# Sixty-one groups of edges fetched by hand instead of fifty-seven, with one semaphore a buffer: a graph network layer on one Trainium2 core

## The chip, the cores and the metric

The kernel runs on one core of one Trainium2 chip. The metric is the time of the whole program on the device, in microseconds (us). A profiled execution has a span as well: the time from its first to its last instruction.

A core has five engines with instruction queues of their own: TensorE (PE, with its weight loads shown as PEld), VectorE (DVE), ScalarE (ACT), GpSimd (POOL) and SyncE (SP). SyncE computes nothing; it issues DMAs. Engines wait for each other by semaphores.

## What is computed

A layer of a graph network over 12,500 nodes with 128 features and 400,000 edges with 32 features, the edges sorted by their target node. The reference, cut to its core:

```python
h = jnp.maximum(_layernorm(x, axis=-1), 0.0)
s, d = src, dst                                      # of 400,000 edges, sorted by d
e = jnp.concatenate([h[s], h[d], edge_attr], axis=-1)
m = jax.nn.relu(e @ w1 + b1) @ w2 + b2
agg = jax.ops.segment_sum(m, d, num_segments=12500)
gi = agg @ w_ih + b_ih
gh = h @ w_hh + b_hh
r, z = sigmoid(i_r + h_r), sigmoid(i_z + h_z)
n = tanh(i_n + r * h_n)
out = x + (1.0 - z) * n + z * h
```

## The kernel before

**Stages.** First the nodes are normalised. The kernel keeps `h` transposed in SBUF (`hT_all`, one column of 128 numbers a node) and writes two products to DRAM: `A = h @ w1[0:128]`, the part of the source node, and `B = h @ w1[128:256] + b1`, the part of the target node. Then the edges pass in 391 groups (`NP`) of up to eight tiles of 128 edges (`PAIR = 8`; 1,024 edges). A group is worked in two units, and the main loop at the end of the kernel runs over the 782 units `u`; a unit of group `k` is `2k` or `2k + 1`.

**One group.** TensorE adds two parts of an edge's row in PSUM (`pre`, L663 on): the target's row of `B` (chosen by a one-hot matrix that `onehot_T` makes from the target numbers) and the edge features. The third part, the source's row of `A`, comes in one of three ways:

- *Gathered.* `gather` (L148) issues eight indirect DMAs on GpSimd, one a tile of 128 rows, into a buffer `G`. There are eleven such buffers (`GBUFS`), taken in a ring, so a gather refills the buffer of the gathered group eleven places earlier, once that one has been used. `add` (L687) adds `G` to PSUM on VectorE, with a floor at zero, and writes `RB` (L701). The first nine groups (`RAW`) are gathered from `x` itself, since `A` isn't ready then; they are normalised here, by VectorE and ScalarE (`raw_stats`, `raw_fin`, `raw_h`, `raw_turn`).
- *As columns.* `one_by_one` copies the columns of the 1,024 source nodes out of `hT_all`, one by one, on ScalarE (`"act"`, L960) or, two at a time with a byte copy behind each 128, on VectorE (`"dve"`, L967 and L972). Each column's place is a register, loaded in lots of 16 or 32 (L945). TensorE then multiplies these columns by `w1[0:128]` (L684), and ScalarE's `relu` writes `RB` (L710).
- *As rows.* SyncE issues one small DMA a row (`"sp"`, L952) from `A` into a buffer `G_sp`, of which there is one. `add` then treats it as a gathered group.

`RB` is summed into target nodes by TensorE (`seg`, L724), with a one-hot of each edge's place in a window of 32 nodes as the weights. `onehot` (L606 on) makes this for one group with one comparison on VectorE (L623), into one of six buffers.

**Who fetches which group.** `SPREAD` says how many groups go to the three engines by hand and `START` the unit in which each engine's first job begins. The list of places runs from `START // 2 + 2` to `NP` less a number for each engine, evenly spaced. Before, VectorE has 27 groups (22, 36, ... 370, 384), ScalarE 28 (17, 31, ... 372, 386) and SyncE 2 (196 and 379); the other 334 are gathered. A job's columns or rows are spread evenly over the units from the job before it to its own group, less four units (eight for SyncE): `run_jobs` issues a part of them in each of four phases of a unit.

**Order.** The order on each engine is written out by hand in the main loop. A unit issues gathers (`gathers`), window rows and loads on SyncE, a part of the jobs, `stages(u)` (which works ahead: the one-hots for three groups later, `pre` for unit `u + 3`, `add` and `relu` for unit `u + 2`), and `seg(u)`. Every engine works through its queue in order.

**Semaphores.** The library gives each DMA a semaphore out of eight lanes for GpSimd's DMAs and eight for SyncE's, in turn. A DMA waits until the DMA before it in its lane has landed. VectorE's add waits for the eight lanes of its group's eight gathers, and for TensorE.

Of the kernel before, what the change touches and what calls it, by code (L numbers as in the profile page):

```python
# [55 lines left out]
SPREAD = {"dve": 27, "act": 28, "sp": 2}  # L56
START = {"dve": 14, "act": 4, "sp": 24}
# [6 lines left out]
def tile_gnn(ctx: ExitStack, tc: tile.TileContext, x, src, srcT, dstT, dstP, eaT, eaP, w1, b1, w2T, b2,  # L64
# [27 lines left out]
    for m, n in SPREAD.items():  # L92
        lo, hi = START[m] // 2 + 2, NP - {"dve": 7, "act": 5, "sp": 12}[m]
        for i in range(n):
            k = lo + int((i + 1) * (hi - lo) / n)
            while k in mode:
                k += 1
            mode[k] = m
            order[m].append(k)
# [47 lines left out]

    def gather(k):  # L148
        if k >= NP or k in mode:
            return  # L150
        G[k] = gp.tile([128, GRP, 2, D], F32, name="G")
        table = x if k < RAW else A
        for u in (2 * k, 2 * k + 1):
            for t, j, a in unit_tiles(u):
                c, i = divmod(t, CH)
                nc.gpsimd.indirect_dma_start(  # L156
                    out=G[k][:, j, a, :], out_offset=None, in_=table,
                    in_offset=bass.IndirectOffsetOnAxis(ap=src_i[c][:, i:i + 1], axis=0))

# [7 lines left out]
    OHB = [const.tile([128, GRP, 2, V], F32, name=f"OH{i}") for i in range(6)]  # L167
# [438 lines left out]
    def onehot(k):  # L606
        if k >= NP:
            return
        t0, t1 = tiles(k)
        OH[k] = OHB[k % len(OHB)]  # L610
        row = SEGB[((k - 3) // 2 + 1) % 2][:, 256:256 + V]
        for a in range(2) if k == 0 else (None,):
            if a is None:
                o, s = OH[k].rearrange("p j a v -> p a j v"), slice(t0, t1)
                d = dloc[:, s].rearrange("p (a j) -> p a j", a=2)[:, :, :, None]
                shape = [128, 2, GRP, V]
                i = row[:, None, None, :]
            else:
                e = min(t1, (a + 1) * GRP)
                o, d = OH[k][:, :e - a * GRP, a, :], dloc[:, a * GRP:e, None]  # L620
                shape = [128, e - a * GRP, V]
                i = row[:, None, :]
            nc.vector.tensor_tensor(o, d.to_broadcast(shape), i.to_broadcast(shape),  # L623
                                    op=ALU.is_equal)
# [62 lines left out]
    def add(u):  # L687
        if u >= NU or u < 0:
            return
        k, h = divmod(u, 2)  # L690
        if h == 0 and k < NP - 1:
            return
        c = slice(0, PAIR) if k < NP - 1 else slice(GRP * h, GRP * h + GRP)
        o, p = RB[k % 2][:, c, :D], PP[k][:, c, :]
        if u in HE or k in hand:
            RT[u] = o, p
            HE.pop(u, None)
            HE.pop(u - 1, None)
            hand.pop(k, None)
        else:  # L700
            nc.vector._custom_dve(TENSOR_ADD_SAT, out=o, in0=p,  # L701
                                  in1=G[k].rearrange("p j a f -> p (j a) f")[:, c, :], s0=float("inf"), s1=0.0)
        if h == 1:
            PP.pop(k)
            G.pop(k, None)
# [9 lines left out]
    def seg(u):  # L715
# [218 lines left out]
    def one_by_one(m, k):  # L934
        et = {"act": ET.Activation, "dve": ET.DVE, "sp": ET.SP}[m]
        r = by_hand.index(k)
        if m == "sp":
            G[k] = pj.tile([128, GRP, 2, D], F32, name="G_sp", bufs=1)
# [4 lines left out]
        for e0 in range(0, PAIR * 128, LOAD[m]):  # L943
# [4 lines left out]
            if m == "sp":  # L948
                for i, v in enumerate(vals):
                    e = e0 + i  # L950
                    a, j = divmod(e // 128, GRP)
                    nc.sync.dma_start(rows[e % 128:e % 128 + 1, j, a, :],  # L952
                                      A_bytes[bass.ds(v, ROW)].rearrange("(o f) -> o f", o=1))
# [316 lines left out]
```

## Time and profile before

| | |
|---|---|
| time, median of 3 runs | 3408.0 us (3399.38 to 3409.23) |
| time of the profiled execution | 3403.76 us |
| span of the profiled execution | 3401.8 us |
| TensorE busy, its granted clock | 2417.4 us, 71%; 0.796 |
| VectorE busy | 2225.1 us, 65% |
| ScalarE busy | 3079.4 us, 91% |
| GpSimd busy | 2566.1 us, 75% |
| DMA, mean | 99 GB/s |

How to read the rows of such a page: a row has the line of the kernel, the engine, the operation, what it writes and reads, the shape, and how often it ran; behind the first bar stand the busy time in us and the mean duration of one in ns; behind the second the idle time of the engine just before these instructions, and what ended most of it. "issue" means that the profile shows nothing that the engine waited for. Register loads, semaphore waits and the issue of DMAs don't count as busy; in a timeline they stand with a q behind the engine's name. In a view of windows a row has the start and end of a stretch and its length, then for each engine the busy time and, in brackets, how many instructions. In a view of waits a row has who waited for whom, the total in us, how often, and the longest.

### The profile page before, as it was taken

Reading aid. Unit: us, or ns where it says so; the run is one execution under the profiler, and the core shown is the slowest. Engines: PE = TensorE matmul, PEld = TensorE weight load, DVE = VectorE, ACT = ScalarE, POOL = GpSimd, SP = SyncE. Lnnn points to the kernel's source line nnn. Section 1 sums busy time; section 2 is a strip of 40 time slices with the busy share of each in tenths; the row PEclk is TensorE's granted clock in tenths of the full one; section 3 lists DMA queues with packets and bytes.
Section 4 is the critical chain, followed back from the end, with each engine's and each line's share of the span. In section 5 each row is a group of like instructions: output and inputs, shape, how many; then the busy total and the mean of one; then the engine's idle time right before and its main releaser. Section 6 shows DMA issues by size and latency. Waiting matters only on the chain. (4 is left out here: it accounts for less than half of the span.)

```text
span 3401.8 us, 88642 instructions
## 1 busy us (share of the span) xinstructions
PE 2417.4 (71%) x13113; PEld 1563.7 (46%) x13113; DVE 2225.1 (65%) x16468; ACT 3079.4 (91%) x29057; POOL 2566.1 (75%) x2678
## 2 busy tenths in 40 slices
PE   7567777777677767776777667676677767766767
PEld 7444444444445444544444444444444434444445
DVE  8556666666676666666666666666666666666665
ACT  7699999999999998999899988988988898898984
POOL 7777777777777777777777777777777777777776
PEclk9777887887887778777877877788777778777878
DMA  6434444434443333343434433443433334343332
GB/s 213 106 88 93 97 100 99 101 94 100 102 98 94 98 99 95 95 101 97 98 93 99 98 94 93 96 96 93 98 93 92 95 94 99 92 97 96 92 92 73
DMA packets 191316, 335.44 MB, mean 99 GB/s; under 512 B 66753, under 2 KB 112384, under 8 KB 190729
## 3 DMA queue, kind: packets, MB, share of 16 engines
q0 software_dynamic: 85408, 175.09, 23.0%
q1 hardware_dynamic: 105177, 154.58, 16.4%
q14 instruction: 478, 3.92, 0.4%
q8 instruction: 109, 1.79, 0.2%
q10 hardware_dynamic: 144, 0.07, 0.0%
HBM read 309.24 MB, written 20.24 MB: 97 GB/s over the span
## 5 line engine op out<-in xcount | busy, mean ns | idle before, releaser
L156 POOL DMA_INDIRECT G<-A,src_i x2600 | 2498.9, 961 | 796.2 <-issue 753.7
L960 ACT COPY HE_act<-hT_all 128x4 uint8 x28672 | 2886.8, 189 | 51.4 <-issue 27.0
L967 DVE SCALAR_TENSOR_TENSOR both<-hT_all 128x4 uint16 x13824 | 1173.4, 153 | 988.5 <-issue 980.7
L673 PE MATMUL pre<-RW,L 128*128 128x256 f32 x3128 | 1132.4, 488 | 229.8 <-DVE RB L701 220.6
L673 PEld LDWEIGHTS pre<-RW,L 128*128 128x128 f32 x3128 | 660.6, 236 | 506.1 <-DVE RB L701 234.0
L724 PE MATMUL seg<-RB,OH 128*32 128x129 f32 x6250 | 603.9, 324 | 380.0 <-DVE RB L701 349.7
L724 PEld LDWEIGHTS seg<-RB,OH 128*32 128x32 f32 x6250 | 333.1, 125 | 820.4 <-DVE RB L701 532.7
L701 DVE CUSTOM_DVE_ANT_0 RB<-pre,G 128x1024 f32<-128x1024 f32 (+1 forms) x326 | 394.5, 1210 | 62.7 <-DMA G<-A,src_i 49.2
L575 DVE TENSOR_SCALAR L<-L,node_of 64x512 f32<-64x512 int32 x382 | 186.7, 489 | 9.7 <-DMA L<-in_dstP 9.4
L719 PE MATMUL seg<-zrow 1*128 1x129 bf16 x196 | 45.3, 231 | 164.4 <-DVE OH L623 164.2
L623 DVE TENSOR_TENSOR OH<-dloc,seg 128x256 f32<-128x256 f16 (+1 forms) x392 | 159.5, 407 | 0.5 <-issue 0.5
L750 PE MATMUL nd<-spot,sums 128*128 128x40 f32 x782 | 116.6, 321 | 1.2 <-DVE sums L733 1.2
L750 PEld LDWEIGHTS nd<-spot,sums 128*128 128x128 f32 x782 | 112.4, 231 | 10.5 <-issue 9.0
L710 ACT ACTIVATE RB<-pre 128x1024 f32<-128x1024 f32 x64 | 65.0, 1015 | 52.4 <-PE pre L684 52.4
L809 ACT ACTIVATE gt<-nd 128x512 f32<-128x512 f32 (+2 forms) x28 | 16.4, 585 | 96.5 <-PE nd L803 96.5
L972 DVE COPY HE_dve<-both 128x512 uint8<-128x512 uint8 x216 | 96.6, 447 | 7.4
L684 PEld LDWEIGHTS pre<-w1a,HE_act 128*128 128x128 f32 x448 | 88.4, 245 | 11.6
L684 PEld LDWEIGHTS pre<-w1a,HE_dve 128*128 128x128 f32 x432 | 87.9, 252 | 12.1
L684 PE MATMUL pre<-w1a,HE_act 128*128 128x128 f32 x448 | 86.4, 327 | 0.0
L684 PE MATMUL pre<-w1a,HE_dve 128*128 128x128 f32 x432 | 85.1, 333 | 0.0
L156 POOL DMA_INDIRECT G<-in_x,src_i x69 | 65.9, 954 | 21.8 <-issue 20.7
L233 PE MATMUL nd<-w1b,hT_all 128*128 128x128 f32 x224 | 45.5, 346 | 43.3 <-DVE xb L835 43.3
(177 smaller groups left out, 1383.9 us busy)
## 6 DMA issues: line engine op xcount, KB each, us to landing
L<-in_dstP SPq DMA_DIRECT2D x195, 256.0 KB
L<-in_eaP SPq DMA_DIRECT2D x195, 256.0 KB
G<-A,src_i POOLq DMA_INDIRECT x2600
G_sp<-A SPq DMA_DIRECT2D x2048, 0.5 KB
RW<-B SPq DMA_DIRECT2D x782, 16.0 KB
xb<-in_x SPq DMA_DIRECT2D x26, 256.0 KB
out<-xb SPq DMA_DIRECT2D x26, 256.0 KB
xs<-in_x SPq DMA_DIRECT2D x11, 512.0 KB
```

Of the source, the lines that this page charges most:

```text
L156: nc.gpsimd.indirect_dma_start(out=G[k][:, j, a, :], out_offset=None, in_=table, in_offset=bass.IndirectOffsetOnAxis(ap=src_i[c][:, i:i + ...
L575: nc.vector.tensor_scalar(o, i, node_of[:, k:k + 1], None, op0=ALU.is_equal)
L623: nc.vector.tensor_tensor(o, d.to_broadcast(shape), i.to_broadcast(shape), op=ALU.is_equal)
L673: nc.tensor.matmul(p[:, 2 * i:2 * i + 2, :], Ls[k // QP][:, c0:c0 + 128], RW[k % 4], start=True, stop=not raw)
L684: nc.tensor.matmul(p[:, 2 * i + a, :], cols, w1a, start=False, stop=n + 1 == len(l) or l[n + 1][1] != j)
L701: nc.vector._custom_dve(TENSOR_ADD_SAT, out=o, in0=p, in1=G[k].rearrange("p j a f -> p (j a) f")[:, c, :], s0=float("inf"), s1=0.0)
L710: nc.scalar.activation(o, p, AF.Relu)
L724: nc.tensor.matmul(p[r0:r0 + V, :D + 1], OH[k][:, j, a, :], RB[k % 2][:, 2 * j + a, :D + 1], start=False, stop=all(b != a for _, _, b in r ...
L750: nc.tensor.matmul(p[:, bass.ds(offs[i], V + SHIFT)], sums[:, slot(b, i), :D], spot[:, i % 2, :], start=False, stop=i == len(offs) - 1)
L960: nc.scalar.copy(he[:, e * 4:e * 4 + 4], column(v))
L967: nc.vector.scalar_tensor_tensor(both[:, (e0 % PIECE + i) // 2, :], column(vals[i + 1]), 256.0, column(vals[i]), op0=ALU.mult, op1=ALU.add)
L972: nc.vector.tensor_copy(he[:, p0 * 4:(p0 + PIECE) * 4].rearrange("p (n c b) -> p n c b", c=2, b=4), both.bitcast(U8).rearrange("p n (b c) ...
```

## The change

- *Fewer gathers.* VectorE takes 28 groups as columns instead of 27 and SyncE 5 groups as rows instead of 2 (87, 160, 233, 306, 379); ScalarE's number stays 28. 330 groups are gathered instead of 334.
- *Columns begin sooner and end later.* The first job of ScalarE begins in unit 2 instead of 4, that of VectorE in unit 10 instead of 14. The last groups with columns are 386 (VectorE) and 388 (ScalarE) instead of 384 and 386.
- *Semaphores of the buffers.* A gather of a group from `RAW` up to the last but one counts up a semaphore of its ring buffer (`filled`), and a row of SyncE one of its group (`brought`). These DMAs leave the lanes: they no longer wait for a lane, and the add waits for one value of one semaphore. In the order of the built program the add had waits for eight lanes and TensorE, and has one for `filled` and one for TensorE; each of SyncE's row copies had a wait for a lane, and has none.
- *One-hots of two groups at once.* One comparison writes the one-hots of groups `2i` and `2i + 1`, 512 elements a partition instead of 256, into one of three buffers of twice the size. The tiles stand in another order in it. The first group and the last have comparisons of their own.

The diff, cut to its core:

```diff
-SPREAD = {"dve": 27, "act": 28, "sp": 2}
-START = {"dve": 14, "act": 4, "sp": 24}
+SPREAD = {"dve": 28, "act": 28, "sp": 5}
+START = {"dve": 10, "act": 2, "sp": 24}
...
-        lo, hi = START[m] // 2 + 2, NP - {"dve": 7, "act": 5, "sp": 12}[m]
+        lo, hi = START[m] // 2 + 2, NP - {"dve": 5, "act": 3, "sp": 12}[m]
...
+    filled = [tc.alloc_semaphore(f"filled{i}") for i in range(GBUFS)]
+    uses, goal = [0] * GBUFS, {}
+
     def gather(k):
         if k >= NP or k in mode:
             return
+        i = ring.index(k) % GBUFS
+        if RAW <= k < NP - 1:
+            uses[i] += 1
+            goal[k] = filled[i], 16 * PAIR * uses[i]
...
-                nc.gpsimd.indirect_dma_start(
+                fetched = nc.gpsimd.indirect_dma_start(
                     out=G[k][:, j, a, :], out_offset=None, in_=table,
                     in_offset=bass.IndirectOffsetOnAxis(ap=src_i[c][:, i:i + 1], axis=0))
+                if k in goal:
+                    fetched.then_inc(goal[k][0], 16)
+                    tc.no_tile_sem_insts.add(fetched.ins.name)
+                    tc.add_to_no_dep_group(f"rows{k}", fetched.ins)
...
-    OHB = [const.tile([128, GRP, 2, V], F32, name=f"OH{i}") for i in range(6)]
+    OHB = [const.tile([128, 2 * PAIR, V], F32, name=f"OH{i}") for i in range(3)]
...
     def onehot(k):
-        if k >= NP:
+        if k >= NP or (k % 2 and k > 1):
             return
...
+        n = 2 if 1 < k < NP - 1 else 1
+        for i in range(n):
+            OH[k + i] = o[:, PAIR * ((k + i) % 2):PAIR * ((k + i) % 2) + PAIR, :]
+        t0, t1 = tiles(k)[0], tiles(k + n - 1)[1]
...
+        for p, e0, e1 in parts:
+            shape = [128, e1 - e0, V]
+            nc.vector.tensor_tensor(p, dloc[:, e0:e1, None].to_broadcast(shape),
+                                    row[:, None, :].to_broadcast(shape), op=ALU.is_equal)
...
         else:
-            nc.vector._custom_dve(TENSOR_ADD_SAT, out=o, in0=p,
+            if k in goal:
+                nc.vector.wait_ge(*goal[k])
+            made = nc.vector._custom_dve(TENSOR_ADD_SAT, out=o, in0=p,
                                   in1=G[k].rearrange("p j a f -> p (j a) f")[:, c, :], s0=float("inf"), s1=0.0)
+            if k in goal:
+                tc.declare_no_dep(made.ins, group=f"rows{k}", reason="behind the wait for the landing")
+                tc.declare_fence(made.ins, group=f"rows{k}")
...
-            nc.tensor.matmul(p[r0:r0 + V, :D + 1], OH[k][:, j, a, :],
+            nc.tensor.matmul(p[r0:r0 + V, :D + 1], OH[k][:, a * GRP + j, :],
...
         if m == "sp":
+            goal[k] = tc.alloc_semaphore(f"brought{r}"), 16 * PAIR * 128
             G[k] = pj.tile([128, GRP, 2, D], F32, name="G_sp", bufs=1)
...
-                    nc.sync.dma_start(rows[e % 128:e % 128 + 1, j, a, :],
-                                      A_bytes[bass.ds(v, ROW)].rearrange("(o f) -> o f", o=1))
+                    fetched = nc.sync.dma_start(rows[e % 128:e % 128 + 1, j, a, :],
+                                                A_bytes[bass.ds(v, ROW)].rearrange("(o f) -> o f", o=1))
+                    fetched.then_inc(goal[k][0], 16)
+                    tc.no_tile_sem_insts.add(fetched.ins.name)
+                    tc.add_to_no_dep_group(f"rows{k}", fetched.ins)
```

More of the change, by code (lines that the diff above doesn't have):

```diff
@@ L606, in onehot @@
     def onehot(k):
-        if k >= NP:
+        if k >= NP or (k % 2 and k > 1):
             return
-        t0, t1 = tiles(k)
-        OH[k] = OHB[k % len(OHB)]
+        o = OHB[(k // 2) % len(OHB)]
         row = SEGB[((k - 3) // 2 + 1) % 2][:, 256:256 + V]
[L612 to L624, printed above, removed]
+        n = 2 if 1 < k < NP - 1 else 1
+        for i in range(n):
+            OH[k + i] = o[:, PAIR * ((k + i) % 2):PAIR * ((k + i) % 2) + PAIR, :]
+        t0, t1 = tiles(k)[0], tiles(k + n - 1)[1]
+        if k:
+            parts = ((o[:, PAIR * (k % 2):PAIR * (k % 2) + t1 - t0, :], t0, t1),)
+        else:
+            parts = tuple((OH[0][:, a * GRP:min(t1, (a + 1) * GRP), :], a * GRP, min(t1, (a + 1) * GRP))
+                          for a in range(2))
+        for p, e0, e1 in parts:
+            shape = [128, e1 - e0, V]
+            nc.vector.tensor_tensor(p, dloc[:, e0:e1, None].to_broadcast(shape),
+                                    row[:, None, :].to_broadcast(shape), op=ALU.is_equal)
     def unit(u):
```

## The prediction

> **What bounds the kernel now.** I read the page first, for the engine that never rests: GpSimd (POOL), which issues the gathers.
>
> ```profile
> PE 2417.4 (71%) x13113; PEld 1563.7 (46%) x13113; DVE 2225.1 (65%) x16468; ACT 3079.4 (91%) x29057; POOL 2566.1 (75%) x2678
> L156 POOL DMA_INDIRECT G<-A,src_i x2600 | 2498.9, 961 | 796.2 <-issue 753.7
> L960 ACT COPY HE_act<-hT_all 128x4 uint8 x28672 | 2886.8, 189 | 51.4 <-issue 27.0
> ```
>
> ScalarE is the busiest by share, yet POOL is the one without slack: the pause before a gather is 796.2/2600 = 0.31 us, nearly all "issue". The view of line 156 gives the first and last start:
>
> ```profile
> L156 POOL DMA_INDIRECT G<-A,src_i x2600: 940/945/1552, 92.3 to 3383.9; - x186
> ```
>
> From 92.3 to 3383.9 + 0.95 = 3384.9 are 3292.6 us for 2600 gathers: **1.266 us each, 10.13 us for a group of eight**, with nothing between. 334 of the 391 groups are gathered.
>
> The second question is who follows whom. Two adds of VectorE (DVE) and the windows between them:
>
> ```profile
> 227.82 1.21 DVE L701 CUSTOM_DVE_ANT_0 RB<-pre,G 128x1024 f32<-128x1024 f32 x1
> 1597.41 1.22 DVE L701 CUSTOM_DVE_ANT_0 RB<-pre,G 128x1024 f32<-128x1024 f32 x1 [0.55 <-DMA G<-A,src_i]
> ...
> 228.00:1598.00 1370.00, 258.38 (x2688) 142.75 (x2688) 175.02 (x145) 24.39 (x24) 0.80 0.40 98
> ...
> 228.00:1598.00 1370.00, 1005.62 (x5429) 638.26 (x5428) 928.29 (x7054) 1310.22 (x12777) 1039.28 (x1082) 0.80 0.40 98
> ...
> DVE both L967 <- issue: 421.0, 374, 2.6
> ...
> DVE RB L701 <- DMA G<-A,src_i: 48.4, 28, 3.7
> ```
>
> The first window counts the writes of RB: 145 adds and 24 relus, so the two adds are 168 groups apart (12 and 180): 8.15 us a group. In the second, VectorE is busy 928.3 of 1370 us; it stands another 421.0 before its column work, waiting for nothing but its own register loads. That is 98.5%: **up to group 180 VectorE sets the pace**, with ScalarE at 95.6% beside it. The last row is of the time after 1598 us: now the adds wait for gathers. The consumer has caught up, and from 1597.41 to the add of group 385 at 3357.91 (below) a group takes 1760.5/205 = 8.59 us, about 10.13 x 334/391 = 8.65: **GpSimd's pace**. As GpSimd never stops in either stage, the end is its work plus a tail of 3401.8 - 3384.9 = 17 us.
>
> **The change, part by part.** *Fewer gathers.* 57 groups fetched by hand become 61 (VectorE 27 to 28, SyncE 2 to 5), so 4 groups, 32 gathers, go: 32 x 1.266 = **-40.5 us**. What was pruned from the waits gives GpSimd nothing by my reading: the earliest gathers, which have no predecessor to wait for, already run at the same 1.25 us:
>
> ```profile
> 4.67 0.94 POOL L156 DMA_INDIRECT G<-in_x,src_i  x1 [0.31 <-issue]
> 5.92 0.94 POOL L156 DMA_INDIRECT G<-in_x,src_i  x1 [0.30 <-issue]
> ```
>
> *One more column group on VectorE.* Its jobs come every 379/28 = 13.54 groups instead of 375/27 = 13.89, 2.6% denser.
>
> ```profile
> 228.00:1598.00 1370.00, 526.71 (x6204) 0.80 0.40 98
> ...
> 228.00:1598.00 1370.00, 43.57 (x97) 0.80 0.40 98
> ...
> L623 DVE TENSOR_TENSOR OH<-dloc,seg 128x256 f32<-128x256 f16 x390 | 159.1, 408 | 0.5 <-issue 0.5
> ...
> L813 DVE TENSOR_TENSOR gt<-gt,misc 128x512 f32<-128x512 f32 x26 | 17.6, 678 | 0.1
> ...
> L701 DVEq EVENT_SEMAPHORE  x1358: 21/50/2846, 201.2 to 3386.5; - x194
> ```
>
> Columns (first row), their byte copies (second) and the loads' 421.0 make 991.3/168 = 5.90 us a group; 2.6% is **+0.15**. One-hots of two groups: 2 x 0.408 becomes one of 512 elements, which no row shows; the 512-element row with an input in PSUM has 0.678, so -0.14 a pair, **-0.07** a group (bounds: nothing, if only the elements count, and -0.2, half of 0.408). The add's eight waits become one: 1358/326 = 4.2 waiting instructions of 50 ns now, one or two after, so -0.13 to 0; I take -0.06. VectorE's own pace becomes 8.15 + 0.15 - 0.07 - 0.06 = 8.17 us (8.02 to 8.30). It lies under the rest only while it stays below the gathers'.
>
> *GpSimd against VectorE.* Gathers last 961 ns in the mean, 945 in the median: 16 ns x 2600 = 42 us of lengthening.
>
> ```profile
> L575 DVE TENSOR_SCALAR L<-L,node_of 64x512 f32<-64x512 int32 x382 | 186.7, 489 | 9.7 <-DMA L<-in_dstP 9.4
> ...
> L972 DVE COPY HE_dve<-both 128x512 uint8<-128x512 uint8 x216 | 96.6, 447 | 7.4
> ```
>
> Put wholly on these 598 instructions it is 0.07 us each; the added column group brings 8 more copies: **+0.6 us**. [...]
>
> *Columns begin sooner.* ScalarE starts at unit 2 instead of 4, VectorE at 10 instead of 14 (a unit is half a group), while the first nine groups are still normalised here. ScalarE's relus mark the pace:
>
> ```profile
> 132.77 1.00 ACT L710 ACTIVATE RB<-pre 128x1024 f32<-128x1024 f32 x1
> 139.33 1.00 ACT L710 ACTIVATE RB<-pre 128x1024 f32<-128x1024 f32 x1
> 148.78 1.00 ACT L710 ACTIVATE RB<-pre 128x1024 f32<-128x1024 f32 x1
> 160.60 1.00 ACT L710 ACTIVATE RB<-pre 128x1024 f32<-128x1024 f32 x1
> ...
> 203.40 0.95 POOL L156 DMA_INDIRECT G<-A,src_i  x1 [0.72 <-DVE RB L701]
> ```
>
> Two units without columns take 6.6 us (132.77 to 139.33), with them 11.8 (148.78 to 160.60): starting two units sooner makes everything behind 5.3 us later. VectorE's four units fall where ScalarE sets the pace; I put 2 us on them (0 to 12). What is late next is GpSimd: a gather refills the buffer of eleven gathered groups ago, and at 203.40 it already waits 0.72 us for group 9's add. So there the 7 us become a stall of GpSimd in full. The first hand-fetched groups also move one or two places forward, which makes some refills depend on an add one group later (8.15 us) where a few us of margin exist: 3 more. **+10 us**, bounds 0 and 25.
>
> *Columns end later.* The last hand-fetched groups are 386 and 388 instead of 384 and 386.
>
> ```profile
> 3351.58 1.02 ACT L710 ACTIVATE RB<-pre 128x1024 f32<-128x1024 f32 x1 [2.24 <-PE pre L684]
> 3357.91 1.23 DVE L701 CUSTOM_DVE_ANT_0 RB<-pre,G 128x1024 f32<-128x1024 f32 x1
> 3366.24 1.02 ACT L710 ACTIVATE RB<-pre 128x1024 f32<-128x1024 f32 x1 [1.38 <-PE pre L684]
> 3369.43 1.22 DVE L701 CUSTOM_DVE_ANT_0 RB<-pre,G 128x1024 f32<-128x1024 f32 x1
> ...
> 3386.64 0.69 DVE L701 CUSTOM_DVE_ANT_0 RB<-pre,G 128x512 f32<-128x512 f32 x1 [3.67 <-DMA G<-A,src_i]
> ```
>
> These are groups 384 to 387 and the last add. Group 385's gathers end 32 before the last, at 3344.4, and its add comes 13.5 us behind; the groups after it have no columns, cost 3.2 us and catch up, so the last add waits for its gather. Afterwards only 24 gathers follow 385, which ends at 3384.9 - 40.5 + 10 - 30.4 = 3324.0. With a lag of 9 there (5 to 13), one group at 8.2, the stretch 386 to 388 at the 14.7 that 384 to 386 take now, and three steps of 3.2, the last add is at 3365.5, against 3386.6 - 40.5 + 10 = 3356.1 by gathers alone: **+9 us** (0 to 13).
>
> *SyncE.* Each row copy no longer waits for one of eight lanes.
>
> ```profile
> 1088.38 1.32 SPq L952 DMA_DIRECT2D G_sp<-A  x4
> 1089.87 0.81 SPq L602 DMA_DIRECT2D RW<-B  x2
> 1090.80 0.58 SPq L563 DMA_DIRECT2D L<-in_dstP  x1
> 1091.43 0.50 SPq L566 DMA_DIRECT2D L<-in_eaP  x1
> 1092.05 1.59 SPq L952 DMA_DIRECT2D G_sp<-A  x4
> ...
> L945 SPq TENSOR_LOAD <-at x64: 1876/2142/2377, 227.6 to 3229.5; - x64
> ```
>
> A job of 1024 rows now has about 68 groups: 15.1 rows x 0.33 = 5.0, their register loads 15.1/32 x 2.14 = 1.0, window rows 0.8, the half of the two L loads 0.5, some 0.3 for nodes: 7.6 of 8.5 us. It stays hidden, with 0.9 us of room a group.
>
> Sum on the profiled execution's own time (span 3401.8, time 3403.8): 3403.8 - 40.5 + 0.6 + 10 + 9 = **3383 us**. That execution lies 4 us under the median shown and inside its runs, so I leave it there.
>
> **The rivals.** *The buffers hold GpSimd throughout*: the early stall recurs at later refills and takes the upper bound, 25, with the tail's 13: 3403.8 - 40.5 + 0.6 + 38 = 3402, no change. For it: the 0.72 us wait; against: the gap between 8.17 and the new 10.13 x 330/391 = 8.55 grows margin by 0.4 us a group. *VectorE becomes the bound*: from 227.8 + 7 at group 12 to the 3324 of group 385 a pace of 8.28 suffices; above it VectorE decides. If loads find less work to hide under (421.0/387 loads = 1.09 us show now, of 2.15) and its pace is 8.45, group 385 is added at 235 + 373 x 8.45 = 3387, and with the present 44 us behind it and 2 around the span: 3433, slower.
>
> ```profile
> L945 DVEq TENSOR_LOAD <-at x864: 2095/2150/3239, 188.2 to 3336.5; - x173
> ```
>
> *SyncE becomes the bound*: from 0.385 us a row its group takes 8.5. At the other row's 1.59/4 = 0.40 it takes 8.7 over 340 groups: 235 + 340 x 8.7 + 33 x 8.15 + 46 = 3508 us. For it: 0.40 was seen; against: that row follows a large L load whose lanes it waited on. *GpSimd's 0.31 us pause is the lane wait*, and goes: then VectorE sets all, 235 + 373 x 8.17 + 46 = 3328. Against it stand the early gathers.
>
> **How the numbers follow.** Forecast 0.68, held buffers 0.10, VectorE 0.08, SyncE 0.10, pause 0.04. The forecast's own range is 3363 (no stall, no tail) to 3402. The wide one takes half of VectorE's case: 3360 to 3415; left out are 0.04, 0.04 and 0.10. Within 0.3% (10 us, about what a measurement of this kernel can tell from no change) is 3398 to 3418: half of the held buffers and a third of VectorE's case, 0.08; faster 0.77; slower 0.15.
>
> **What would show it.** Right: gathers still 1.27 us apart, 2637 of them; a new idle stretch of GpSimd of 5 to 20 us in total between 130 and 420 us; adds waiting for gathers only after group 200; the last add not waiting for its gather. Wrong: GpSimd idle beyond 420 us (buffers or VectorE), SyncE's row copies above 0.385 us with adds waiting on G_sp, or gathers closer than 1.25 us.

## The result, and the profile after

The changed kernel takes 3414.53 us (median of 15 runs, 3410.7 to 3423.64) against 3408.0 (15 runs, 3399.38 to 3409.83): a ratio of 1.0024, interval 1.0017 to 1.0031. It was forecast at 3383; it is 6.5 us slower than before. The profiled execution took 3417.5 us, its span is 3415.5.

The page of the changed kernel, first the busy times, then three groups (line 163 is the gather, 713 the add, 986 VectorE's column copies):

```profile
PE 2432.2 (71%) x13129; PEld 1567.2 (46%) x13129; DVE 2255.9 (66%) x16793; ACT 3081.9 (90%) x29058; POOL 2537.3 (74%) x2646
...
L163 POOL DMA_INDIRECT G<-A,src_i x2568 | 2470.1, 962 | 796.5 <-issue 761.1
L986 DVE SCALAR_TENSOR_TENSOR both<-hT_all 128x4 uint16 x14336 | 1213.0, 154 | 1003.3 <-issue 989.9
L713 DVE CUSTOM_DVE_ANT_0 RB<-pre,G 128x1024 f32<-128x1024 f32 x322 | 389.4, 1210 | 16.8 <-PE pre L683 16.8
```

The last row holds the answer: the adds wait 16.8 us in all, and none of it for gathered rows. Before, they waited for gathers 48.4 us after 1598 us alone. The consumer never catches up with GpSimd.

GpSimd itself did what was forecast. The view of line 163 (shortest, median and longest duration in ns, then the first and last start), and the timeline of GpSimd around the buffers' first refill:

```profile
L163 POOL DMA_INDIRECT G<-A,src_i x2568: 941/947/1812, 93.1 to 3355.5; - x198
...
196.92 1.19 POOL L163 DMA_INDIRECT G<-A,src_i  x1 [2.42 <-PE misc L666]
214.25 0.95 POOL L163 DMA_INDIRECT G<-A,src_i  x1 [7.13 <-DVE RB L713]
```

The gathers end at 3355.5 + 0.95 = 3356.4; the forecast's terms give 3384.9 - 40.5 + 10 = 3354.4. The stall is there, 7.1 us behind an add and 2.4 behind a TensorE product. (The add of group 12 comes 11.5 us later than before, at 239.27 instead of 227.82, where the forecast had 7.) But the tail behind the last gather is 3415.5 - 3356.4 = 59 us, where the forecast had 17 + 9 = 26. These 33 us are nearly the whole miss (3417.5 - 3383 = 34.5).

In the timeline of VectorE, the adds of groups 12, 176 and 378, and the last three:

```profile
239.27 1.21 DVE L713 CUSTOM_DVE_ANT_0 RB<-pre,G 128x1024 f32<-128x1024 f32 x1
1629.01 1.21 DVE L713 CUSTOM_DVE_ANT_0 RB<-pre,G 128x1024 f32<-128x1024 f32 x1
3317.20 1.22 DVE L713 CUSTOM_DVE_ANT_0 RB<-pre,G 128x1024 f32<-128x1024 f32 x1
...
3390.39 1.22 DVE L713 CUSTOM_DVE_ANT_0 RB<-pre,G 128x1024 f32<-128x1024 f32 x1 [1.51 <-PE pre L683]
3395.31 1.29 DVE L713 CUSTOM_DVE_ANT_0 RB<-pre,G 128x512 f32<-128x512 f32 x2 [3.14 <-PE pre L683]
```

The pace is (1629.01 - 239.27)/164 = **8.47 us** a group, then (3317.20 - 1629.01)/202 = 8.36. The forecast's own bound was 8.28: above it VectorE decides. The last add waits for TensorE, not for its gather.

To split the pace, I take VectorE's own work between the adds of groups 12 and 176: its busy time, and the idle time before column copies that nothing released (the loads). The window and the view of VectorE's waits, first before, with the add of group 176 ahead:

```profile
1564.69 1.21 DVE L701 CUSTOM_DVE_ANT_0 RB<-pre,G 128x1024 f32<-128x1024 f32 x1
...
227.80:1564.70 1336.90, 984.17 (x5314) 624.16 (x5314) 907.27 (x6891) 1277.94 (x12455) 1014.18 (x1056) 0.80 0.40 98
...
DVE both L967 <- issue: 409.5, 364, 2.6
```

and after, with VectorE's longest waits on other engines and TensorE's longest:

```profile
239.30:1629.00 1389.70, 1003.07 (x5314) 629.28 (x5314) 916.15 (x6974) 1269.59 (x12334) 1055.22 (x1097) 0.78 0.41 96
...
DVE both L986 <- issue: 421.2, 353, 2.6
DVE RB L713 <- PE pre L683: 14.9, 6, 3.9
DVE TOT L776 <- PE nd L765: 9.9, 2, 6.5
...
PE seg L739 <- DVE RB L713: 128.9, 72, 5.4
```

Before, (907.27 + 409.5)/164 = 8.03 us of the 8.15 are own work. After, (916.15 + 421.2)/164 = 8.16 of 8.47. So the own work grew by 0.13, and the rest, which is nearly all waiting for other engines and DMAs, from 0.12 to 0.32. For the two together the forecast had +0.02. From group 176 to 378, where before is held by the gathers, the changed kernel has 8.21 us of own work (1124.1 busy and 534.5 before columns in 202 groups) and 0.15 of waits.

### The profile page after: what moved, and what is told of

It reads as the page before. It is cut to its first block, busy times and chain, and to the rows that moved or that the text cites. A ratio compares the mean times of both kernels' runs of the same rounds, so it can differ in the third digit from the quotient of the medians.

```text
span 3415.5 us, 93943 instructions
## 1 busy us (share of the span) xinstructions
PE 2432.2 (71%) x13129; PEld 1567.2 (46%) x13129; DVE 2255.9 (66%) x16793; ACT 3081.9 (90%) x29058; POOL 2537.3 (74%) x2646
## 3 DMA queue, kind: packets, MB, share of 16 engines
q14 instruction: 518, 4.24, 0.4%
## 5 line engine op out<-in xcount | busy, mean ns | idle before, releaser
L163 POOL DMA_INDIRECT G<-A,src_i x2568 | 2470.1, 962 | 796.5 <-issue 761.1
L979 ACT COPY HE_act<-hT_all 128x4 uint8 x28672 | 2890.5, 189 | 53.9 <-issue 29.8
L986 DVE SCALAR_TENSOR_TENSOR both<-hT_all 128x4 uint16 x14336 | 1213.0, 154 | 1003.3 <-issue 989.9
L683 PEld LDWEIGHTS pre<-RW,L 128*128 128x128 f32 x3128 | 667.8, 238 | 507.4 <-issue 296.1
L739 PE MATMUL seg<-RB,OH 128*32 128x129 f32 x6250 | 616.3, 329 | 336.6 <-DVE RB L713 296.2
L713 DVE CUSTOM_DVE_ANT_0 RB<-pre,G 128x1024 f32<-128x1024 f32 x322 | 389.4, 1210 | 16.8 <-PE pre L683 16.8
L633 DVE TENSOR_TENSOR OH<-dloc,seg 128x512 f32<-128x512 f16 (+1 forms) x198 | 132.3, 668 | 0.1
L765 PE MATMUL nd<-spot,sums 128*128 128x40 f32 x782 | 125.5, 335 | 5.7 <-DVE sums L748 5.7
L765 PEld LDWEIGHTS nd<-spot,sums 128*128 128x128 f32 x782 | 121.0, 246 | 15.2 <-issue 9.0
L694 PEld LDWEIGHTS pre<-w1a,HE_dve 128*128 128x128 f32 x448 | 78.5, 219 | 8.7
L848 PE MATMUL nd<-ident,gt 128*128 128x128 f32 (+2 forms) x112 | 29.6, 412 | 71.5 <-DVE gt L844 67.1
```

The lines of the kernel that those rows point to most:

```text
L163: fetched = nc.gpsimd.indirect_dma_start(out=G[k][:, j, a, :], out_offset=None, in_=table, in_offset=bass.IndirectOffsetOnAxis(ap=src_i[c] ...
L633: nc.vector.tensor_tensor(p, dloc[:, e0:e1, None].to_broadcast(shape), row[:, None, :].to_broadcast(shape), op=ALU.is_equal)
L683: nc.tensor.matmul(p[:, 2 * i:2 * i + 2, :], Ls[k // QP][:, c0:c0 + 128], RW[k % 4], start=True, stop=not raw)
L694: nc.tensor.matmul(p[:, 2 * i + a, :], cols, w1a, start=False, stop=n + 1 == len(l) or l[n + 1][1] != j)
L713: made = nc.vector._custom_dve(TENSOR_ADD_SAT, out=o, in0=p, in1=G[k].rearrange("p j a f -> p (j a) f")[:, c, :], s0=float("inf"), s1=0.0)
L739: nc.tensor.matmul(p[r0:r0 + V, :D + 1], OH[k][:, a * GRP + j, :], RB[k % 2][:, 2 * j + a, :D + 1], start=False, stop=all(b != a for _, _, ...
```

## The experiments

Theory: VectorE's pace, raised by the 28th column group, holds the kernel. Rivals: SyncE's fuller queue (late window rows), the early beginning, or the semaphores and one-hots themselves. ScalarE, which was at 95.6% before, is busy 1269.59 of 1389.70 us in the window above, 91%, so it is not the one. The first four runs shared one chip (before: 3406.18 us there), the next four another (3399.02), so each is compared by its ratio to before. The table gives pace, own work and the rest per group from add 12 to add 176, worked out as above from unrounded figures, one profile a kernel; rows follow where a verdict rests on them.

| kernel | ratio [interval] | pace | own | waits |
|---|---|---|---|---|
| before | 1 | 8.15 | 8.03 | 0.12 |
| changed | 1.0024 [1.0017, 1.0031] | 8.47 | 8.16 | 0.32 |
| old split and places | 1.0011 [1.0002, 1.0021] | 8.14 | 7.91 | 0.22 |
| SyncE 2 groups | 1.0013 [1.0004, 1.0023] | 8.43 | 8.14 | 0.30 |
| VectorE 27 groups | 0.9940 [0.9923, 0.9956] | 8.26 | 7.89 | 0.37 |
| old beginnings and ends | 1.0020 [1.0010, 1.0029] | 8.46 | 8.25 | 0.22 |
| half the loads | 0.9915 [0.9899, 0.9932] | 8.25 | 6.35 | 1.89 |
| half of each add | 0.9915 [0.9898, 0.9931] | 8.28 | 8.01 | 0.27 |
| single one-hots | 1.0045 [1.0030, 1.0059] | 8.44 | 8.13 | 0.31 |
| gathers in lanes | 1.0184 [1.0156, 1.0211] | 8.52 | 8.27 | 0.25 |

**The semaphores and one-hots alone.** The changed kernel with

```diff
-SPREAD = {"dve": 28, "act": 28, "sp": 5}
-START = {"dve": 10, "act": 2, "sp": 24}
+SPREAD = {"dve": 27, "act": 28, "sp": 2}
+START = {"dve": 14, "act": 4, "sp": 24}
...
-        lo, hi = START[m] // 2 + 2, NP - {"dve": 5, "act": 3, "sp": 12}[m]
+        lo, hi = START[m] // 2 + 2, NP - {"dve": 7, "act": 5, "sp": 12}[m]
```

> The change's semaphores and one-hots of two groups alone; the groups by hand and their places as before (27, 28, 2). 334 groups are gathered, so GpSimd bounds the second half as before. By the prediction's own terms for these two edits (-0.07 and -0.06 us a group) the pace from group 12 to 176 falls from 8.15 to about 8.02 us, and the time stays within 6 us of before (3408). If the two edits save VectorE nothing, the pace is 8.15 again. Neither theory of the slowdown (SyncE's full queue, VectorE's further column group) expects late window rows here: TensorE's waits for RW stay under 20 us in the whole run.

Its window and waits of VectorE up to group 176, and over the whole span the wait for gathers:

```profile
228.50:1563.00 1334.50, 981.54 (x5314) 621.93 (x5314) 899.26 (x6808) 1279.10 (x12461) 1013.22 (x1052) 0.80 0.39 98
...
DVE both L986 <- issue: 398.4, 341, 2.4
DVE RB L713 <- DMA G<-A,src_i: 12.5, 5, 3.5
...
DVE RB L713 <- DMA G<-A,src_i: 107.5, 46, 6.6
```

VectorE's own work falls by 0.12, (899.26 + 398.4)/164 = 7.91, as summed, but the pace is 8.14, not the expected 8.02. This is the gathers' doing: from 1300 us on the adds wait for them (12.5 us in the window). Up to group 130 no add does, and there the pace is (1173.6 - 228.5)/118 = 8.01 against (1184.7 - 227.8)/118 = 8.11 before: 0.10 of the forecast's 0.13 arrive. ScalarE is busy 96% of the window; whether it holds the rest no run tells. In the second half the adds wait for gathers throughout, so nothing is gained. Alone these parts leave the time where it was, +0.1%.

**SyncE's queue.** The changed kernel with 2 groups on SyncE:

```diff
-SPREAD = {"dve": 28, "act": 28, "sp": 5}
+SPREAD = {"dve": 28, "act": 28, "sp": 2}
```

> The change with SyncE at 2 groups instead of 5; 333 groups are gathered. SyncE theory (rows fill its queue, window rows land late, TensorE and then VectorE wait): TensorE's waits for RW fall from 86 us to under 20, the pace from group 12 to 176 falls from 8.47 to 8.2, GpSimd becomes the bound again after some 250 groups and the time is about 3405 (gathers end near 3386, a tail of some 20). VectorE theory (its own work is too long): the pace stays at 8.4 or above and the time at 3412 to 3420.

TensorE's waits for window rows of SyncE, over the span, in this kernel:

```profile
PE pre L683 <- DMA RW<-B: 10.6, 1, 10.6
```

and in the changed kernel:

```profile
PE pre L683 <- DMA RW<-B: 85.9, 25, 10.1
```

They are gone, and the pace stays at 8.43 with the same 0.30 of waits. SyncE isn't what holds it, and three groups more to gather (30 us of GpSimd) cost no time either: GpSimd has that much room.

**VectorE's 28th group.** The changed kernel with 27 column groups:

```diff
-SPREAD = {"dve": 28, "act": 28, "sp": 5}
+SPREAD = {"dve": 27, "act": 28, "sp": 5}
```

> The change with VectorE at 27 groups instead of 28, SyncE still at 5; 331 groups are gathered. VectorE theory: the pace from group 12 to 176 falls from 8.47 to 8.25 or less, the gathers (ending near 3367) bound the end, and the time is 3385 to 3392. SyncE theory: waits for RW stay at 50 us or more, the pace stays at 8.35 or above, and the time is 3400 or more.

3385.11 us: 0.6% faster than before on the same chip, and by the ratios 0.8% faster than the changed kernel. Its window, its column copies in it (x5996; the changed kernel has 6220 in its window), the waits there and the wait for gathers over the span:

```profile
232.80:1586.90 1354.10, 978.80 (x5298) 617.75 (x5297) 893.18 (x6748) 1269.50 (x12332) 1028.13 (x1070) 0.79 0.41 97
...
232.80:1586.90 1354.10, 507.24 (x5996) 0.79 0.41 97
...
DVE both L986 <- issue: 400.2, 327, 2.6
...
DVE RB L713 <- DMA G<-A,src_i: 55.4, 27, 4.3
```

The pace drops to 8.26, under 8.28, and the adds wait for gathers again. SyncE's theory fails a second time: TensorE's waits for window rows are 172.6 us over the span, twice those of the changed kernel, and the kernel is faster. Own work falls by 8.16 - (893.18 + 400.2)/164 = 0.27 us for (6220 - 5996)/164 = 1.37 column copies a group: 0.196 us each, or 0.27/1.37 x 512 = 100 us for a job, where the forecast used the average, 5.90/36.9 x 512 = 82.

Behind this stands one profile of each kernel; with the own work of the kernel with 2 groups on SyncE, which has the same columns as the changed one, it is 0.184 us and 94.

Why the margin costs more than the average can be read from VectorE's queue. The timeline of the changed kernel, and the register loads of its column line:

```profile
1509.27 0.50 DVE L991 COPY HE_dve<-both 128x512 uint8<-128x512 uint8 x1
1511.52 1.28 DVE L986 SCALAR_TENSOR_TENSOR both<-hT_all 128x4 uint16 x16 [1.76 <-issue]
1512.72 0.47 DVE L586 TENSOR_SCALAR L<-L,node_of 64x512 f32<-64x512 int32 x1
1514.30 1.02 DVE L986 SCALAR_TENSOR_TENSOR both<-hT_all 128x4 uint16 x12 [1.10 <-issue]
...
L961 DVEq TENSOR_LOAD <-at x896: 2095/2152/3206, 176.1 to 3364.1; - x180
```

Sixteen copies take 1.28 us; then the queue loads 32 registers for 2.15. Whatever VectorE is still working on covers a part of it: here 0.47 us of line 586 stands under the second load. By this reading the cover is fixed, so a further job finds less of it; halving the adds (below) bears it out. Paid in full a job is 32 x 2.15 + 512 x 0.08 + 8 x 0.45 = 113 us. The measured 94 to 100 lie between that and 82.

**The early beginning.** The changed kernel with the beginnings and ends of before:

```diff
-START = {"dve": 10, "act": 2, "sp": 24}
+START = {"dve": 14, "act": 4, "sp": 24}
...
-        lo, hi = START[m] // 2 + 2, NP - {"dve": 5, "act": 3, "sp": 12}[m]
+        lo, hi = START[m] // 2 + 2, NP - {"dve": 7, "act": 5, "sp": 12}[m]
```

> The change with the columns' first units and last places as before (first jobs in units 14 and 4, last groups 384 and 386). Both theories: the add of group 12 comes 11 us sooner (228 instead of 239), GpSimd's idle time before group 22's gather (7.1 us) goes. As the consumer and not GpSimd bounds the end of the changed kernel, the time falls by these 11 us, to 3403, if the pace stays at 8.47; if beginning sooner was worth its price, denser jobs bring the pace to 8.5 or above and the time stays at 3412 to 3418.

The add of group 12 in this kernel:

```profile
227.07 1.22 DVE L713 CUSTOM_DVE_ANT_0 RB<-pre,G 128x1024 f32<-128x1024 f32 x1
```

It comes 12.2 us sooner than with early columns, but the time is not the expected 11 us less. Up to group 176 the pace is the same, though the same jobs lie closer (own work 8.25 instead of 8.16). The lead is lost behind: from group 176 to 378 own work is 8.35 instead of 8.21 and the pace 8.45 instead of 8.36, 19 us in 202 groups. (The profiled execution was the slowest of ten, 3420.09 us; their median is 3412.71.) So beginning early isn't what made the changed kernel slower.

**Half of the register loads**, in the changed kernel; each place is used for two columns, so half of the columns are those of other nodes:

```diff
-                at[r:r + 1, e0:e0 + LOAD[m]], engines=[et], min_val=low, max_val=high,
+                at[r:r + 1, e0:e0 + LOAD[m] // (2 if m == "dve" else 1)], engines=[et], min_val=low, max_val=high,
...
+            vals = list(vals) * (2 if m == "dve" else 1)
```

> The change with half of VectorE's register loads left out: each lot loads 16 places instead of 32 and uses each for two columns, so half of its columns are other nodes' columns. All instructions of the columns stay. If VectorE's own work is the bound, by its queue or by its total, the pace from group 12 to 176 falls from 8.47 to under 8.1, adds wait for gathers in the second half again, and the time is the gathers' end (3356 or earlier) and a tail of 17 to 28 us: 3370 to 3386. If waits between the engines hold the pace whatever VectorE does, the pace stays at 8.3 or above and the time at 3400 or more.

Waits of VectorE and TensorE up to group 176, and of VectorE for gathers over the span:

```profile
DVE L L586 <- DMA L<-in_dstP: 200.0, 55, 10.6
DVE both L987 <- issue: 126.1, 226, 1.4
...
PE pre L683 <- DMA RW<-B: 333.3, 65, 10.2
...
DVE RB L713 <- DMA G<-A,src_i: 235.0, 67, 8.2
```

VectorE's own work falls by 1.8 us a group, the pace by only 0.23, to 8.25 where under 8.1 was expected. Now SyncE's loads (`L`, `RW`) come late: the second bound lies right behind the first (the forecast had left SyncE 0.9 us a group of room). With half of each add and with 27 groups the pace is 8.28 and 8.26, as if by the same bound. But 8.25 is under 8.28, so GpSimd sets the end.

**Half of each add**, in the changed kernel; the other half of the sums is left out:

```diff
-            made = nc.vector._custom_dve(TENSOR_ADD_SAT, out=o, in0=p,
-                                  in1=G[k].rearrange("p j a f -> p (j a) f")[:, c, :], s0=float("inf"), s1=0.0)
+            part = slice(0, GRP) if k in goal else slice(None)
+            made = nc.vector._custom_dve(TENSOR_ADD_SAT, out=o[:, part, :], in0=p[:, part, :],
+                                  in1=G[k].rearrange("p j a f -> p (j a) f")[:, c, :][:, part, :], s0=float("inf"), s1=0.0)
```

> The change with half of each add left out (four tiles of eight; the other half of the sums is not made), 0.69 instead of 1.21 us. Total theory (VectorE's busy time and its visible load time add up): 0.52 us less for 0.845 adds a group, so the pace falls by 0.44 to about 8.03, GpSimd bounds the end and the time is 3375 to 3386. Queue theory (VectorE's instruction queue is the bound, held 2.15 us by each register load, and an add runs beneath a load): the idle time before columns grows by what the adds lose, the pace falls by less than 0.15 and the time stays at 3400 or more.

Its window and VectorE's wait for loads:

```profile
238.70:1596.90 1358.20, 980.83 (x5314) 618.43 (x5314) 844.81 (x6974) 1269.14 (x12334) 1030.41 (x1076) 0.80 0.41 97
...
DVE both L987 <- issue: 469.4, 398, 2.7
```

Busy time falls by (916.15 - 844.81)/164 = 0.43 us a group, but the idle time before columns grows by (469.4 - 421.2)/164 = 0.29: two thirds of what the adds gave up shows as load. So adds run largely beneath the loads, and the queue rather than the arithmetic is VectorE's limit. The pace falls by 0.19, to 8.28: less than the 0.44 by which busy time and loads would simply add up, a little more than the 0.15 that the queue theory allowed. It suffices to come to the bound of 8.28, so the time falls, which the queue theory had not expected.

In both of these runs the ratio is 0.9915, 3379 us on 3408.0: **the forecast's 3383 within 4 us, once VectorE is out of the way.** With 27 groups on VectorE one group more is gathered, 10.1 us, and the ratio is 0.0025 x 3400 = 8.5 us higher.

**One-hots of one group each**, as before the change, in the changed kernel:

```diff
-    OHB = [const.tile([128, 2 * PAIR, V], F32, name=f"OH{i}") for i in range(3)]
+    OHB = [const.tile([128, GRP, 2, V], F32, name=f"OH{i}") for i in range(6)]
...
-        if k >= NP or (k % 2 and k > 1):
+        if k >= NP:
...
-            nc.tensor.matmul(p[r0:r0 + V, :D + 1], OH[k][:, a * GRP + j, :],
+            nc.tensor.matmul(p[r0:r0 + V, :D + 1], OH[k][:, j, a, :],
```

> The change without its one-hots of two groups: each group has a comparison of its own again, in one of six buffers. By the prediction's term the pace rises by 0.07 to 8.54 and the time, bound by the consumer, by 373 x 0.07 = 26 us to 3440. Queue theory: a comparison runs beneath a load, its saving is one handing-over of some 0.07 us for two groups, and the time rises by 0 to 15 us (3414 to 3430).

The comparison in the changed kernel over the span, by its page:

```profile
L633 DVE TENSOR_TENSOR OH<-dloc,seg 128x512 f32<-128x512 f16 (+1 forms) x198 | 132.3, 668 | 0.1
```

One of 512 elements takes 0.668 us against 2 x 0.408: 0.07 us a group less, as estimated. Yet own work is 8.13 with single ones and 8.16 with double ones. The time saved is filled by waiting for loads, as in the run before. The time itself is 0.2% above the changed kernel's by the ratios, about 7 us, within the 0 to 15 that the queue theory gave (its 0.07 us for a handing-over was an estimate; VectorE's column copies start a median of 0.073 us apart in the kernel before) and far from the 26 of the prediction's term; their intervals just touch.

**The gathers back in their lanes**, so that the adds wait for eight of them again:

```diff
-        if RAW <= k < NP - 1:
+        if False:
```

> The change without the buffers' semaphores of the gathers: the gathers are in lanes again and each add waits for eight lanes by four waiting instructions; SyncE's rows keep their own semaphores. By the prediction's term (0.06 us a group) the pace rises to 8.53 and the time by 22 us to 3437. Queue theory: the three waiting instructions more for an add pass through the queue in about 0.1 us each, 0.25 us a group, so the pace rises to 8.7 and the time by 90 us to 3500. If the waits cost nothing the time stays at 3414.

Its windows (to group 176, and from there to 378), VectorE's wait for loads in the first, and GpSimd's waits for buffers over the span:

```profile
239.10:1636.00 1396.90, 995.56 (x5314) 626.61 (x5314) 921.82 (x6975) 1271.38 (x12338) 1054.54 (x1102) 0.79 0.40 96
1636.00:3353.00 1717.00, 1196.21 (x6538) 757.02 (x6538) 1126.97 (x8557) 1569.59 (x15075) 1298.23 (x1356) 0.80 0.40 96
...
DVE both L986 <- issue: 433.7, 376, 2.2
...
POOL G L163 <- DVE RB L713: 25.3, 19, 7.7
```

Own work is 8.27, 0.11 more than with one semaphore a buffer (forecast: 0.06; the 0.1 us of the queue theory is how far apart the waiting instructions of an add start in the kernel before, a median of 0.098 us), and the kernel 1.8% slower than before. The pace up to group 176 is 8.52, as the prediction's term has it (8.53). But the second half loses as well (1717.0/202 = 8.50 against 8.36), so the time, 3471 us by the ratio, lies midway between the 3437 of that term and the 3500 of the queue theory. GpSimd isn't what holds it: it waits 25.3 us for buffers in all. Without the semaphores 28 groups on VectorE would have been a clear loss.

**What the split with 27 groups is made of.** Four more kernels start from 27 column groups: with the old beginnings and ends, with 2 groups on SyncE, with half of SyncE's row copies (below; every second row is left out), and once more unchanged.

```diff
+                    if i % 2:
+                        if i % STEP[m] == STEP[m] - 1:
+                            yield
+                        continue
...
-                    fetched = nc.sync.dma_start(rows[e % 128:e % 128 + 1, j, a, :],
-                                                A_bytes[bass.ds(v, ROW)].rearrange("(o f) -> o f", o=1))
+                    fetched = nc.sync.dma_start(rows[e % 128:e % 128 + 2, j, a, :],
+                                                A_bytes[bass.ds(v, ROW)].rearrange("(o f) -> o f", o=1).to_broadcast([2, ROW]))
```

> The changed kernel with 27 column groups on VectorE (as before the change), and the columns' beginnings and ends as before the change; SyncE keeps 5 groups. Theory (with 27 column groups VectorE's pace is under what the gathers need, so GpSimd's work and its early stall set the end): the stall of about 10 us near 200 us is gone, the add of group 12 comes at 227 us instead of 232.8, the gathers end about 10 us earlier than with 27 groups and early columns, and the ratio to before is 0.991 to 0.992 instead of 0.994. Rival (an early beginning is repaid by less dense jobs, as with 28 groups): the denser jobs put VectorE's pace up to group 176 from 8.26 to 8.3 or more and the ratio is 0.994 or above.

> The changed kernel with 27 column groups on VectorE and 2 row groups on SyncE: the same split as before the change, but with the semaphores of the buffers, the one-hots of two groups and the early columns. 334 groups are gathered instead of 331. Theory (GpSimd sets the end with 27 column groups): three groups more at 10.13 us are 30 us more than with SyncE's 5, a ratio of 1.003 (1.001 to 1.005), though VectorE's own pace falls to 7.9 and waits for window rows are under 20 us in all. Rival (SyncE's fuller queue takes back most of what its three groups save): the ratio stays at 0.994 to 0.998.

> The changed kernel with 27 column groups on VectorE; SyncE issues only every second row copy of its 5 groups, each to two partitions (every second row of these groups is left out, the one before it stands in its place). 331 groups are gathered as with all rows. Theory (with 27 groups GpSimd sets the end; SyncE's queue holds the pace only up to the middle, where there is slack): waits of TensorE for window rows fall from 173 us to under 30, the pace up to group 176 falls from 8.26 to 8.1 or less, and the time stays: ratio 0.993 to 0.995. Rival (SyncE's late loads are the next bound for the whole time too): the ratio falls to 0.991 or below.

> The changed kernel with 27 column groups on VectorE once more, on the chip of the three runs beside it. Theory: ratio 0.994 again (0.992 to 0.996), the gathers back to back from 250 us on and the adds waiting for them in the second half. If that run had profited from its chip, the ratio would be 0.998 or above.

All four came to a third chip, where the kernel before itself took 5665.76 us (12 runs, 5626.98 to 5678.66). Repeated with the same expectations they came to two others, at 5664.42 and 5713.85. The ratios there, in the order of the chips: old beginnings 1.0123, 1.0120, 1.0080; 2 groups on SyncE 1.0119, 1.0115, 1.0105; half the rows 1.0078, 1.0102; 27 groups once more 1.0167 [1.0134, 1.0199] and 1.0149 [1.0126, 1.0172]. The page of the last kernel on the first of these chips shows another bound:

```profile
L979 ACT COPY HE_act<-hT_all 128x4 uint8 x28672 | 3157.3, 190 | 2212.6 <-issue 2186.4
L163 POOL DMA_INDIRECT G<-A,src_i x2576 | 2467.1, 958 | 3077.1 <-DVE RB L713 2198.0
```

ScalarE stands 2186 us before its column copies, waiting for nothing that the profile shows (29.8 in the changed kernel), and GpSimd waits 2198 us for VectorE. TensorE's granted clock is 0.67 there, against 0.80 in the runs of 3400 us. So none of the expectations was tested; what SyncE's groups and the old beginnings are worth beside 27 column groups stays open. The version with 27 groups is the best one only where before takes its 3400 us; on these chips it is 1.5 to 1.7% slower than before.

## Why the prediction was wrong

The forecast said faster, for GpSimd's work. The rival "VectorE becomes the bound", given 0.08, is what happened. Its pace of 8.45 was met up to group 176 (8.47) and not behind it (8.36), so it cost less than the 3433 it was given. That 3414.5 us lies just inside the stated range is no credit to the forecast: the range was widened for half of this rival.

- *Fewer gathers, -40.5, and the early stall, +10:* right. The gathers end 2.0 us from where these terms put them.
- *Columns denser, +0.15 a group:* too small. It took a job at its average cost. At the margin it is 0.18 to 0.20 us a column copy (27 against 28 groups), for one more copy a group as much; from the old split and places to the changed kernel own work grows by 0.24, in which SyncE's groups and the new beginnings lie too. The rival had named the reason, less to hide loads under, and the profile had its two numbers (1.09 us of a load's 2.15 showing); the sum still took the average.
- *One-hots, -0.07, and waits pruned, -0.06:* their sum was right (with these parts alone own work falls by 0.12, and the pace by 0.10 where no add waits for gathers), the split was not: by the kernels with single one-hots and with lanes 0 and -0.11.
- *VectorE's pace, 8.17 in the sum:* **this step failed**; it is 8.47. Of the missing 0.30, 0.11 are own work (+0.13 instead of +0.02). The other 0.20 are waits, nearly all of VectorE on other engines (0.12 before, 0.32 after), for which the sum had no term: it took the 1.5% of waits as given.
  - The semaphores and one-hots are not what failed: with them alone the pace up to group 130 falls by 0.10 of 0.13.
  - What was mis-sized is the +0.15 of the further column group, with nothing for SyncE's groups and the new places beside it: from the old split and places to the changed kernel the pace up to group 130 rises from 8.01 to (1241.3 - 239.3)/118 = 8.49. Taken out of the changed kernel one by one, the column group gives back 0.18 of these 0.48, SyncE's three groups 0.05 and the places 0.01. The other half comes only from their being together; the kernel that would show which two it takes, 27 groups with SyncE at 2, ran only on the chips of 5700 us.
  - The longest of the waits are for TensorE's products. TensorE in turn waits for VectorE, but no longer for its adds than before (139.5 us then, 128.9 now). SyncE isn't the cause of the waits, since they stay at 0.30 with its queue light. TensorE's granted clock isn't either: in these windows it is 0.78 in the changed kernel and with the old beginnings, 0.79 with 27 groups, and the waits are 0.32, 0.22 and 0.37; over whole runs the kernel with the old beginnings had the clock of before on the same chip, 0.80, and was 0.2% slower all the same. Why the waits grew by this much stays open; that they and the own work made the time is shown by the kernels that relieve VectorE.
- *The bound of 8.28:* it holds as far as the runs go. The kernels at 8.28 and below end with GpSimd, and those at 8.43 and above don't; none lies between.
- *Columns end later, +9:* too large, though inside its bounds. In the changed kernel the tail of 59 us is the consumer's lag. In the three kernels that have the later ends and end with GpSimd (27 groups, half the loads, half of each add) the last gather ends at 3361.6, 3349.3 and 3349.4 and the span at 3382.3, 3370.4 and 3369.7: a tail of 20 to 21 us against 17, so about +4.
- *SyncE hidden:* its 7.6 us are right. (In its rival, 0.385 us a row gives 8.4 by the same sum, not 8.5.) With gaps of more than 0.3 us in its queue counted as rest, the records give 90% of the changed kernel's window and 92% of that with half the loads, 7.6 us a group in both. But room in the mean doesn't make its loads punctual: with half the loads they hold VectorE and TensorE at 8.25 us a group. A row copy costs what was estimated, 0.33 us; the timeline of SyncE's queue has 1.87 us for six:

```profile
999.98 1.87 SPq L968 DMA_DIRECT2D G_sp<-A  x6
```

- *+0.6 us of VectorE's copies against GpSimd:* no run shows this term; that 598 instructions of VectorE carry the whole lengthening of the gathers was the author's estimate. The gathers' mean is 962 ns, before 961, their median 947 and 945: the lengthening is (962 - 947) x 2568 = 39 us beside 382 + 224 = 606 such instructions, and was 42 us beside 598. The term itself is too small to be seen: 0.6 us in 2568 gathers is 0.2 ns each.

Of the signs that the forecast named for being right, most came: the gathers start 1.27 us apart, there are 2637 of them, and the stall lies between 130 and 420 us. The last add doesn't wait for its gather either, but because VectorE is 40 us late (3396.6 against 3356.4), not because of late columns. One sign failed, and it is the one that tells who follows whom: the adds never waited for gathers. The sign named for VectorE as the bound, GpSimd idle beyond 420 us, did not come at all: the longest wait of a gather for an add is 0.3 us there. It could not come at such paces, for 8.47 and 8.36 are still under the 8.55 that the gathers take for a group. VectorE gains on GpSimd all the way: the add of group 12 starts 105 us after its gathers have ended (134.3 us), that of group 378 52 us after (3265.3), and the last ends 40 us after. It just doesn't catch up before the end, which is what the bound of 8.28 says.

## What to carry to other kernels

Before a further job is put on an engine whose own queue sets the pace, price it at what the queue pays for it, loads and waits included, and not at the visible average: here the cover that made the earlier jobs cheap did not grow with the jobs. Compare the resulting pace with the one at which the next bound takes over; here 0.2 us a group lay between a gain of 0.6% and a loss of 0.2%. And where engines are as close as here (98.5 and 95.6% before, and SyncE's loads behind them), don't take a change of one engine's work for the change of the pace: here 0.13 us more of VectorE's own work came with 0.32 more of pace, and 1.8 less with only 0.23 less. A consumer that starts far behind can set the end although it is faster than its producer (8.36 against 8.55 here): what counts is whether it catches up in time, and that shows in its own waits for data, not in the producer's.

## What the runs showed of the hardware

Arithmetic that ran beneath register loads cost VectorE much less here than its busy time: halving the adds took 0.43 us a group of busy time away and put 0.29, two thirds of it, on the waiting before columns, and 0.07 us less of comparisons a group left its own work where it was (8.16 and 8.13).

On three chips of the five that served the experiments, the kernel before took two thirds longer: 5664 to 5714 us, against 3399 and 3406 on the other two. ScalarE's timeline there (27 groups, first of these chips) has stretches in which one or two copies come 0.7 us (1500.90 to 1501.61) or 1.4 us (1501.61 to 1503.03) before the next, beside others in which 68 take 6.79 us, as in the changed kernel (69 in 7.02 us):

```profile
1500.90 0.19 ACT L979 COPY HE_act<-hT_all 128x4 uint8 x1 [0.51 <-issue]
1501.61 0.29 ACT L979 COPY HE_act<-hT_all 128x4 uint8 x2 [0.52 <-issue]
1503.03 0.29 ACT L979 COPY HE_act<-hT_all 128x4 uint8 x2 [1.13 <-issue]
...
1507.33 6.79 ACT L979 COPY HE_act<-hT_all 128x4 uint8 x68 [0.52 <-issue]
```

VectorE stands longer as well, 1665.5 us before its column copies against 989.9 in the changed kernel. The register loads last as long on the other two of these chips as in the changed kernel (a median of 2150 and 2151 ns on VectorE against 2152), so they aren't the cause. The DMA queue that the pages call "instruction" moves as much on the first of them as in the changed kernel on a chip of 3400 us, 514 packets and 4.21 MB against 518 and 4.24, and its packets take no larger share of the span (0.2 and 0.4%). What holds ScalarE there, no run tells.
